# One folded projection for layer 1's first attention, and the 3x3 weights mixed on two engines

## The chip, the cores and the metric

The kernel runs on one core of one Trainium2 chip. The metric is the device time of that core in microseconds (us). The core has engines that run at once, each with its own queue of instructions that it works through in order: TensorE (PE, matrix products; its weight loads are listed apart as PEld), VectorE (DVE), ScalarE (ACT), GpSimd (POOL) and SyncE (SP, which here only starts transfers). GpSimd also starts transfers. Operands lie in SBUF, products land in PSUM.

## The reference

The input is x, (2, 256, 64, 64) in float32: two images ("batches") of 256 channels. Two layers each add something to x.

```python
x = x + layer0(gn(x))      # gn: group norm, 32 groups
x = x + layer1(gn(x))
```

Layer 0 is softmax attention with 8 heads over all 4096 positions. Layer 1, cut to what matters here:

```python
q = c1x1(x, conv1_w, conv1_b); k = c1x1(x, conv2_w, conv2_b); v = c1x1(x, conv3_w, conv3_b)
pos = tile(c1x1(loc, convp_w, convp_b))          # loc: column and row position, -1 to 1
fq = q * 64 ** -0.5 + pos
fk = k + pos
ctx = sa(blockify(fq), blockify(fk), blockify(v))     # 64 groups of 64 positions; the first attention
feats = bn_relu(c1x1(ctx, lr_W_w), ...)
qx, kx = two bn_relu(c1x1) each, of feats; vx = c1x1(feats, sr_fv_w)
out_att = bn_relu(c1x1(sa(qx, kx, vx), sr_W_w), ...)  # 64 groups again; the second attention
f_conv = mix of q, k, v by fc_w                       # 9 x 64 channels
out_conv = depthwise 3x3 of f_conv with dep_w
return rate1 * out_att + rate2 * out_conv
```

`sa` is softmax(q^T k * 256 ** -0.5) v. Within a group of 64 positions, a score is the product of one position's fq and another's fk. Adding to a position's scores a number that doesn't depend on the second position leaves its softmax unchanged. The mix by `fc_w` and the 3x3 behind it are linear in x, so both are one 3x3 over x whose weights follow from conv1_w, conv2_w, conv3_w, fc_w and dep_w.

## The kernel before, in words

Each batch is worked through in turn (the loop at L1245): the norm and projections of layer 0, the attention of layer 0 (`attention0`, over 1000 us of PE work a batch), then layer 1 in two parts. Channels lie on the 128 partitions in KC = 2 chunks; positions are cut into NT = 8 tiles of T = 512. Tile pools give out buffers: "w4" has 11 for working tiles, "wp" three for 256x256 matrices, PSUM eight banks in the first part of layer 1 and four in the second, beside four for the 3x3 (`pacc`).

**The first attention**, `layer1_first` (L1031). `to_groups` writes the normalised input into `xg`, ordered by group, so that `source(t)` gives tile t's 512 positions (8 groups) and all channels. `project` (L1064) multiplies it by w1 and by w2 (L1072) and adds bias and position by one more product of 16 rows, `st_posq` or `st_posk` with the tile's `loc` (L1076); for each of q and k and both 128-channel halves m that makes five products. ScalarE, and in batch 1 for k VectorE, copies q and k to SBUF. `group_attention` (L949) is a generator: scores `sp` (L977), each of 64x64, values `pvs` (L960), the softmax on VectorE with the exponential on ScalarE (L985 to L992); then, after the first `yield`, the transposes `at` (L997) and VectorE's copies `bd` (L1006); after the second, the context `pc` (L1015), which ScalarE turns into `feats` (L1026). `layer1_first` calls `project(t + 1, 0)` and `project(t + 1, 1)` at the two yields, so PE projects the next tile while VectorE works on this one's softmax. In float32 a product is two passes in the records.

**The 3x3's weights**, `conv_weights` (L760), run once, in batch 0. After some small preparation (L791 to L808), for both halves m of the output channels each of nine taps is a weighted sum of 12 rows of `wx` (128x256 each), a TENSOR_SCALAR (L818) and eleven SCALAR_TENSOR_TENSORs (L820), all on VectorE. Then come sums of taps for a transformed 3x3 with 16 weights in place of nine (L824 to L831), and a write to `wf_kept` in DRAM (L833). The two halves share `wx`, `taps` and `new_rows`, so the second loads its `wx` when the first is done with them.

**The second part**, `layer1_second` (L1146), works tile by tile: a q branch of two products (L1186, L1194), a k branch, the second attention, and in between steps of the 3x3, `conv()`: `conv_transform` on GpSimd (L884, L888) and `conv_step` on PE (L898) with its sums on VectorE (L904 to L925). In all there are 16 such steps. `fetch_conv_weights` (L845) loads `wf` and, in batch 0, turns its blocks with PE (L857). It is called at tile 0, and the steps go 3, 3, 2, 2, 2, 2, 2, 0 over the tiles. `results` holds each tile's output until the 3x3 has covered its rows.

**What sets the order.** In `with tc.manual_schedule(engines=...)` the named engines keep the order of the code; in the loop over tiles of the first attention, and in the second part, that is PE alone. The order of the other engines' queues is laid down before the run by a planner that takes an instruction when it expects it to be ready, earlier code first. So `conv_weights`, which comes after the attention in the code, fills VectorE's gaps between the softmax's instructions. `issue_after(done.ins)` (L1142) keeps it behind the last normalisation.

Of the kernel before, what the change touches and what calls it, by code (L numbers as in the profile page):

```python
# [17 lines left out]
P = 128  # L18
B, C, H, W = 2, 256, 64, 64
N = H * W  # L20
T = 512
# [19 lines left out]
def direct_layers(ctx: ExitStack, tc: tile.TileContext, a: dict, out: bass.AP, bad: bass.AP):  # L41
# [36 lines left out]

    ident = const.tile([P, P], F32, name="ident")
# [47 lines left out]
    def load_layer1():  # L127
# [5 lines left out]


        posk, posq = w4([4, C], "posk"), w4([4, C], "posq")
        nc.gpsimd.dma_start(out=posk, in_=a["posk"])
        nc.gpsimd.dma_start(out=posq, in_=a["posq"])
        rows = const.tile([4, 1], F32, name="pos_rows")
        nc.gpsimd.memset(rows, 8.0)
        nc.gpsimd.memset(rows[0:1, :], 1.0)  # L140
        nc.vector.tensor_scalar(posq, posq, rows, None, ALU.mult)
        def stack(name, rows):
            wts[name] = const.tile([16, C], F32R, name="st_" + name)
# [11 lines left out]
        later.append(lambda: (lambda: stack("posq", posq)))  # L155
        later.append(lambda: (lambda: stack("posk", posk)))
# [13 lines left out]
    kept_w = {name: dram.tile([P, KC, C], F32, name="kept_" + name) for name in ("w3", "fv")}  # L170
# [12 lines left out]
    def stack_positions(t):  # L183
# [14 lines left out]
        return halves_of  # L198

# [560 lines left out]
    def conv_weights():  # L760
# [49 lines left out]
        for m in range(2):  # L810
            for q in range(3):
                nc.gpsimd.dma_start(out=wx[:, 4 * q : 4 * q + 4, :], in_=a["wx"][q, m].rearrange("i p c -> p i c"))
            for tap in range(9):
                acc = taps[:, tap, :]
                for i in range(12):
                    src, s = wx[:, i, :], weff[:, m, i, tap : tap + 1]
                    if i == 0:
                        nc.vector.tensor_scalar(acc, src, s, None, ALU.mult)  # L818
                    else:
                        nc.vector.scalar_tensor_tensor(acc, src, s, acc, ALU.mult, ALU.add)  # L820
# [128 lines left out]
    def group_attention(nm, q, k, tokens, wv, out, busy=False, apart=False):  # L949
# [19 lines left out]
        if apart:  # L969
            values(0)  # L970

        sp = bank([P, 4, 64], f"sp_{nm}")
        for t in range(4):
            for c in range(KC):
                for par in range(2):
# [3 lines left out]
                        start=c == 0, stop=c == KC - 1,  # L979
                    )  # L980
        if not apart:
            values(0)
# [48 lines left out]
    def layer1_first(b, xts, put, check, st):  # L1031
# [19 lines left out]
        tiles, banks = {}, {}  # L1051
# [4 lines left out]
        def open_tile(t):  # L1056
            nt = f"lr_{b}_{t}"
            loc = w4([16, T], f"loc_{nt}", F32R)
            nc.sync.dma_start(
                out=loc.bitcast(F32), in_=loc_kept[:, :, :, t * T : (t + 1) * T].rearrange("l d r n -> (l d r) n")  # L1060
            )
            tiles[t] = loc, w4([P, KC, T], f"q_{nt}"), w4([P, KC, T], f"k_{nt}")

        def project(t, m, chunks):  # L1064

            loc, q, k = tiles[t]
            for nm, wt, pos, dst in (("q", "w1", "posq", q), ("k", "w2", "posk", k)):
                if chunks.start == 0:
                    banks[t, m, nm] = bank([P, T], f"p{nm}_lr_{b}_{t}_{m}")
                acc = banks[t, m, nm]  # L1070
                for c in range(chunks.start, chunks.stop):
                    nc.tensor.matmul(  # L1072
                        acc, wts[wt][:, c, m * P : (m + 1) * P], source(t)[:, c, :], start=c == 0, stop=False
                    )
                if chunks.stop == KC:
                    nc.tensor.matmul(acc, wts[pos][:, m * P : (m + 1) * P], loc, start=False, stop=True)  # L1076
                    if nm == "q":
                        nc.scalar.activation(dst[:, m, :], acc, AF.Copy, scale=0.125)
                    elif b == 0:
                        nc.scalar.copy(dst[:, m, :], acc)  # L1080
                    else:
                        nc.vector.tensor_copy(dst[:, m, :], acc)
# [5 lines left out]
        with tc.manual_schedule(engines={E.PE, E.Activation, E.DVE}):  # L1088
# [26 lines left out]
            open_tile(0)  # L1115
            for m in range(KC):
                project(0, m, slice(0, 1))
            for m in range(KC):
                project(0, m, slice(1, KC))
        with tc.manual_schedule(engines={E.PE}):  # L1120
            for t in range(NT):
# [5 lines left out]

                parts = group_attention(
# [697 lines left out]
```

## Time and profile before

Three runs took 3211.84 us (median; 3209.8 to 3215.32). The profile is of one further execution.

| | |
|---|---|
| profiled execution | 3213.2 us |
| its span, first to last instruction | 3211.4 us |
| mean granted clock of TensorE | 0.989 of full speed |
| PE busy | 3093.3 us, 96% |
| VectorE busy | 2487.2 us, 77% |
| ScalarE busy | 2316.5 us, 72% |
| GpSimd busy | 826.7 us, 26% |

Line numbers (L1072) are lines of the kernel before. In a timeline each row is a start in us, a length, the engine, the line, the operation, output<-inputs by the program's names, shape and count; in brackets stands the idle time ahead of it and what ended that. Several like instructions in a row are merged to one. A length can exceed the distance to the next start, since instructions overlap at their ends. A window's row gives the busy time of each engine in a stretch.

### The profile page before, as it was taken

To read this page: it belongs to the slowest core of one execution; us is meant where nothing else is said; L and a number is where in the kernel's file an instruction comes from. 1 tells how busy PE (TensorE), PEld (TensorE's weight loads), DVE (VectorE), ACT (ScalarE), POOL (GpSimd) and SP (SyncE) were. 2 spreads that over 40 slices of the span, in tenths; PEclk is the share of its full clock that TensorE was granted. 3 is DMA by queue.
4 is the path that set the end of the run, shared out by engine and by line. 5 is a ranking of instruction groups with operands and counts; after the bars stand their busy time and mean duration, and the time that the engine had idled before them with its cause. 6 is when DMAs were issued, how large, how long until landed. Compare 5 with 4: busy or idle time off the path is not lost. (4 is left out here: it accounts for less than half of the span.)

```text
span 3211.4 us, 62287 instructions
## 1 busy us (share of the span) xinstructions
PE 3093.3 (96%) x24889; PEld 1838.3 (57%) x24889; DVE 2487.2 (77%) x3223; ACT 2316.5 (72%) x2371; POOL 826.7 (26%) x918
## 2 busy tenths in 40 slices
PE   7899999999999989699998999999999999899998
PEld 4455555555555545466754555555555555456766
DVE  4599998999999988664445899889999999724543
ACT  2699999999999963422235999999999999724222
POOL 2122222222222210344200222222222222104530
PEclk9999999999999999899999999999999999999999
DMA  7968789689786741310049696897887966500000
GB/s 255 258 132 170 157 156 182 138 166 175 155 178 130 149 101 50 131 33 27 27 174 270 129 183 139 159 173 144 172 168 159 191 130 129 143 3 11 20 14 21
DMA packets 242957, 425.73 MB, mean 133 GB/s; under 512 B 99009, under 2 KB 110361, under 8 KB 240225
## 3 DMA queue, kind: packets, MB, share of 16 engines
q0 software_dynamic: 96176, 240.42, 39.0%
q1 hardware_dynamic: 146480, 181.25, 21.0%
q8 instruction: 197, 3.23, 0.4%
q14 instruction: 104, 0.84, 0.1%
HBM read 118.78 MB, written 67.86 MB: 58 GB/s over the span
## 5 line engine op out<-in xcount | busy, mean ns | idle before, releaser
L519 DVE TENSOR_TENSOR e<-e,es 128x1024 f32<-128x1024 f32 (+1 forms) x952 | 1035.9, 1142 | 96.9 <-ACT es L472 95.1
L482 PE MATMUL av<-es,v 128*32 128x256 f32 (+1 forms) x9644 | 747.6, 390 | 0.0
L519 DVE TENSOR_TENSOR e<-e,v 128x1024 f32<-128x1024 f32 (+1 forms) x640 | 675.9, 1108 | 54.4 <-ACT v L472 53.0
L472 ACT ACTIVATE es<-sa 128x1536 f32<-128x1536 f32 (+1 forms) x444 | 635.6, 1432 | 94.9 <-PE sa L466 54.2
L466 PE MATMUL sa<-q,k 128*128 128x512 f32 x1736 | 561.2, 430 | 13.0 <-issue 4.5
L482 PE MATMUL av<-v 128*32 128x256 f32 (+1 forms) x6228 | 506.9, 389 | 0.0
L482 PEld LDWEIGHTS av<-es,v 128*32 128x32 f32 x9644 | 316.5, 109 | 299.7 <-issue 161.3
L466 PEld LDWEIGHTS sa<-q,k 128*128 128x128 f32 x1736 | 280.0, 188 | 296.5 <-issue 142.4
L466 PE MATMUL sc<-q,k 128*128 128x512 f32 x1180 | 372.3, 397 | 10.1 <-ACT es L472 8.5
L466 PE MATMUL sb<-q,k 128*128 128x512 f32 x1180 | 371.1, 395 | 1.3 <-ACT es L472 1.3
L482 PEld LDWEIGHTS av<-v 128*32 128x32 f32 x6228 | 216.7, 109 | 179.3 <-issue 82.2
L472 ACT ACTIVATE es<-sc 128x1024 f32<-128x1024 f32 x296 | 306.9, 1037 | 7.8 <-DMA v<-es 7.8
L472 ACT ACTIVATE v<-sc 128x1024 f32<-128x1024 f32 x294 | 304.8, 1037 | 1.0 <-DMA acc<-v 1.0
L472 ACT ACTIVATE es<-sb 128x1024 f32<-128x1024 f32 x296 | 302.1, 1021 | 4.0 <-DMA acc<-es 3.9
L472 ACT ACTIVATE v<-sb 128x1024 f32<-128x1024 f32 x294 | 300.0, 1020 | 0.5 <-DMA acc<-v 0.5
L466 PEld LDWEIGHTS sc<-q,k 128*128 128x128 f32 x1180 | 210.3, 188 | 82.4 <-ACT es L472 21.0
L466 PEld LDWEIGHTS sb<-q,k 128*128 128x128 f32 x1180 | 221.0, 188 | 56.1 <-ACT es L472 3.5
L472 ACT ACTIVATE v<-sa 128x1536 f32<-128x1536 f32 (+1 forms) x146 | 209.2, 1433 | 35.0 <-PE sa L466 14.9
L898 PE MATMUL mm<-v,wf 128*128 128x256 f32 x1024 | 229.5, 382 | 3.7 <-DVE z L907 3.7
L529 POOL DMA_DIRECT2D es<-es x118 | 101.2, 858 | 484.8 <-ACT es L472 438.2
L888 POOL TENSOR_TENSOR v<-col 128x512 f32<-128x512 f32 x128 | 162.7, 1300 | 237.2 <-PE sp_sr L977 82.3
L898 PEld LDWEIGHTS mm<-v,wf 128*128 128x128 f32 x1024 | 194.4, 191 | 38.4 <-issue 7.7
(243 smaller groups left out, 3254.2 us busy)
## 6 DMA issues: line engine op xcount, KB each, us to landing
acc<-es POOLq DMA_DIRECT2D x130, 512.0 KB, 6.4
acc<-v POOLq DMA_DIRECT2D x84, 512.0 KB, 6.3
es<-es POOLq DMA_DIRECT2D x138, 256.0 KB, 4.3
v<-es POOLq DMA_DIRECT2D x134, 256.0 KB, 5.1
k<-wk_halves SPq DMA_DIRECT2D x64, 512.0 KB
q<-wq_halves SPq DMA_DIRECT2D x256, 128.0 KB
v<-v POOLq DMA_DIRECT2D x90, 256.0 KB, 5.0
es<-v POOLq DMA_DIRECT2D x86, 256.0 KB, 4.0
```

Source lines behind the costliest of these rows:

```text
L466: nc.tensor.matmul(sc[:, i, :], held["k", g // 2][:, j * P : (j + 1) * P], held["q", g, u // 2][:, u % 2, :], start=True, stop=True,)
L472: nc.scalar.activation(dst, sc[:, i : i + m, :], AF.Exp, scale=SC0)
L482: nc.tensor.matmul(dst[HD0 * u : HD0 * u + HD0, n], lhs, rhs(u)[:, n], start=start, stop=stop)
L519: nc.vector.tensor_add(dst[:, s, :], dst[:, s, :], src)
L529: nc.gpsimd.dma_start(out=dst, in_=src, accum_op=ALU.add)
L888: (nc.gpsimd.tensor_add if plus else nc.gpsimd.tensor_sub)(dst, rows(one), rows(two))
L898: nc.tensor.matmul(mm[:, m, r, :], wf[:, k, 4 * r + q, m * P : (m + 1) * P], v[r // 2][:, r % 2, k, :], start=k == 0, stop=k == KC - 1,)
```

## The change

**One projection.** In place of q and k there is y: the matrix g is formed once from w1 and w2, y = g applied to the input (plus position and bias rows), and the scores are products of y with the normalised input itself, `source(t)`. What the position adds on the keys' side needs two numbers a query, `ats`, which `at_grid` computes for four tiles at once, 32 columns each; `more` multiplies them by the group's positions (`grid`) onto the scores. Terms that are the same for all keys of a query are left out. `fold_scores` computes g at the start of batch 0 and keeps it in DRAM for batch 1. The plain w1 and w2 that it needs come row by row out of `wx`. Position loads go two tiles at a time.

**3x3 weights on two engines.** Taps 6, 7 and 8 are mixed on GpSimd, by a multiplication and an addition for each row; the other six stay on VectorE.

**A tile later.** In batch 0 `fetch_conv_weights` moves from tile 0 to tile 1, and the steps go 0, 3, 3, 3, 3, 2, 2, 0. Batch 1 keeps its steps.

```diff
     x_first = load_x(0)
+    by_out = {}
+    for name in ("w1", "w2"):
+        by_out[name] = wpool.tile([P, KC, C], F32, tag="wp", name=f"{name}_by_out")
+        for i in range(4):
+            for half in range(2):
+                r = 64 * (i % 2) + 32 * half
+                nc.sync.dma_start(
+                    out=by_out[name][r : r + 32, i // 2, :], in_=a["wx"][int(name == "w2"), half, i, 0:P:4, :]
+                )
+    place_rows = const.tile([4, C], F32, name="place_rows")
+    nc.sync.dma_start(out=place_rows, in_=a["posq"])
...
-        posk, posq = w4([4, C], "posk"), w4([4, C], "posq")
...
-        later.append(lambda: (lambda: stack("posq", posq)))
-        later.append(lambda: (lambda: stack("posk", posk)))
+        later.append(lambda: (lambda: stack("pos", wts["pos_rows"])))
...
+    def fold_scores():
+        wts["g"] = wpool.tile([P, KC, C], F32, tag="wp", name="wt_g_0")
...
+        for k in range(KC):
+            nc.tensor.transpose(pp[:, k, :], place_rows[:, k * P : (k + 1) * P], ident[0:4, 0:4])
+        nc.scalar.copy(place, pp)
+        pl = bank([4, C + 2], "pt_rows")
+        for dst, src in ((pl[:, 0:C], by_out["w2"]), (pl[:, C : C + 2], place[:, :, 1:3])):
+            for j in range(KC):
+                nc.tensor.matmul(dst, place[:, j, :], src[:, j, :], start=j == 0, stop=j == KC - 1)
+        nc.scalar.activation(rows[:, 0 : C + 2], pl, AF.Copy, scale=scale)
+        for k in range(KC):
+            pg = bank([P, C + 2], f"pt_g_{k}")
+            for dst, src in ((pg[:, 0:C], by_out["w2"]), (pg[:, C : C + 2], place[:, :, 1:3])):
+                for j in range(KC):
+                    nc.tensor.matmul(
+                        dst, by_out["w1"][:, j, k * P : (k + 1) * P], src[:, j, :], start=j == 0, stop=j == KC - 1
+                    )
+            nc.scalar.copy(wts["g"][:, k, :], pg[:, 0:C])
+            nc.scalar.copy(w_at[:, k, 0:2], pg[:, C : C + 2])
+        nc.sync.dma_start(out=kept_w["g"], in_=wts["g"])
...
-            for tap in range(9):
-                acc = taps[:, tap, :]
+            for tap in (6, 0, 1, 7, 2, 3, 8, 4, 5):
+                acc, term = taps[:, tap, :], new_rows[:, 0, :]
                 for i in range(12):
                     src, s = wx[:, i, :], weff[:, m, i, tap : tap + 1]
-                    if i == 0:
+                    if tap >= 6:
+                        nc.gpsimd.tensor_mul(acc if i == 0 else term, src, s.to_broadcast([P, C]))
+                        if i:
+                            nc.gpsimd.tensor_add(acc, acc, term)
+                    elif i == 0:
                         nc.vector.tensor_scalar(acc, src, s, None, ALU.mult)
                     else:
                         nc.vector.scalar_tensor_tensor(acc, src, s, acc, ALU.mult, ALU.add)
...
-        if apart:
+        first = apart or more and more[2]
+        if first:
             values(0)
...
-                        start=c == 0, stop=c == KC - 1,
+                        start=c == 0, stop=not more and c == KC - 1,
                     )
+            for par in range(2 if more else 0):
+                n0 = (4 * par + t) * 64
+                nc.tensor.matmul(
+                    sp[64 * par : 64 * par + 64, t, :], more[0][:, n0 : n0 + 64], more[1], start=False, stop=True
+                )
...
+            for c in range(chunks.start, chunks.stop):
+                nc.tensor.matmul(
+                    acc, wts["g"][:, c, m * P : (m + 1) * P], source(t)[:, c, :], start=c == 0, stop=False
+                )
+            if chunks.stop == KC:
+                nc.tensor.matmul(acc, wts["pos"][:, m * P : (m + 1) * P], loc_of(t), start=False, stop=True)
+                nc.scalar.activation(tiles[t][:, m, :], acc, AF.Copy, scale=0.125)
+        ats = cpool.tile([P, 2, T], F32, tag="col", name=f"at_{b}")
+        def at_grid(half):
+            pa = bank([P, T], f"pa_{b}_{half}")
+            for c in range(KC + 1):
+                for u in range(4):
+                    t, dst = 4 * half + u, pa[HD0 * u : HD0 * u + HD0, :]
+                    if c < KC:
+                        nc.tensor.matmul(dst, w_at[:, c, :], source(t)[:, c, :], start=c == 0, stop=False)
+                    else:
+                        nc.tensor.matmul(
+                            dst, wts["pos"][:, C : C + HD0].bitcast(F32), loc_of(t).bitcast(F32), start=False, stop=True
+                        )
+            nc.scalar.activation(ats[:, half, :], pa, AF.Copy, scale=0.125)
...
+            at_grid(0)
...
+                if t == 3:
+                    at_grid(1)
...
+        steps = (0, 3, 3, 3, 3, 2, 2, 0) if b == 0 else (3, 3, 2, 2, 2, 2, 2, 0)
...
-                if t == 0:
+                if t == steps.index(max(steps)):
                     wf = fetch_conv_weights(b)
-                if t + 1 < NT:
+                if steps[t] > 0:
                     conv()
...
-                if t + 1 < NT:
+                if steps[t] > 1:
                     conv()
...
-                if t < 2:
+                if steps[t] > 2:
                     conv()
...
+            if b == 0:
+                fold_scores()
...
-        load_set(b, ("w1", "w2", "w3"))
+        load_set(b, ("w3",) if b == 0 else ("g", "w3"))
```

## The prediction

> **What bounds the kernel now.** I read the page's first two parts, then the busy time of each stretch, then the timelines of TensorE, VectorE and GpSimd where the diff works. TensorE (PE) is busy 96% of the span. The stretches below are: up to batch 0's first attention of layer 1, that attention, the gap behind it, the rest of batch 0's layer 1, batch 1 up to its first attention, that attention, the end. Columns: window, length, then busy time (and instructions) of PE, PEld, DVE, ACT, POOL, the clock, DMA.
>
> ```profile
> 0.00:1180.10 1180.10, 1136.97 (x10444) 646.84 (x10444) 1019.27 (x1086) 1019.15 (x994) 307.15 (x395) 0.99 0.80 170
> 1180.10:1314.40 134.30, 130.63 (x688) 76.86 (x688) 121.71 (x342) 54.87 (x79) 3.04 (x9) 0.99 0.15 40
> 1314.40:1346.00 31.60, 7.40 (x17) 2.88 (x17) 16.96 (x12) 10.99 (x16) 25.53 (x16) 0.70 0.49 179
> ...
> 2788.00:2921.90 133.90, 130.47 (x688) 76.98 (x688) 42.53 (x91) 41.94 (x56) 0.79 (x6) 0.99 0.03 8
> ```
>
> Both first attentions are PE's: 134 us each, 130 busy. In batch 0 VectorE (DVE) is nearly as full, 121.7 of 134.3 us, as it also mixes the 3x3's weights; GpSimd (POOL) is empty. In the gap PE has 7.4 us of work in 31.6. PE's timeline for one tile of batch 0, then for the gap (start, length, what, idle before and its releaser):
>
> ```profile
> 1207.89 1.15 PE L977 MATMUL sp_lr<-k_lr,q_lr 128*64 128x64 f32 x32
> 1208.97 3.72 PE L960 MATMUL pvs_lr<-wt_w,xg 128*128 128x256 f32 x16
> 1212.53 1.88 PE L1072 MATMUL pq_lr<-xg,wt_w 128*128 128x512 f32 x4
> 1214.34 0.49 PE L1076 MATMUL pq_lr<-loc_lr,st_posq 16*128 16x512 f32 x1
> 1214.76 1.98 PE L1072 MATMUL pk_lr<-xg,wt_w 128*128 128x512 f32 x4
> 1216.67 0.49 PE L1076 MATMUL pk_lr<-loc_lr,st_posk 16*128 16x512 f32 x1
> 1217.10 0.44 PE L997 MATMUL at_lr<-ident,e_lr 128*128 128x128 f32 x2
> ...
> 1346.00 9.61 PE L857 MATMUL pw<-ident,wf 128*128 128x128 f32 x64 [23.79 <-DMA wf<-wf_kept]
> ```
>
> Tiles follow each other every 16.03 us (sp_lr at 1207.89 and 1223.92) with no idle. The second block's 23.79 us wait is for the finished 3x3 weights: their last sums, VectorE's L831, ended at 1331.36. Why they ended so late is the reading that decides my forecast. VectorE's last sums first alone (1251), then beside GpSimd's TENSOR_TENSORs, which are listed after them:
>
> ```profile
> 1251.86 1.09 DVE L831 TENSOR_TENSOR prep<-prep 128x256 f32<-128x256 f32 x3
> ...
> 1323.41 3.77 DVE L830 TENSOR_TENSOR prep<-prep 128x256 f32<-128x256 f32 x2
> 1327.10 4.26 DVE L831 TENSOR_TENSOR prep<-prep 128x256 f32<-128x256 f32 x3
> ...
> 1318.52 6.09 POOL L888 TENSOR_TENSOR v<-col 128x512 f32<-128x512 f32 x4
> 1326.97 5.50 POOL L888 TENSOR_TENSOR v<-col 128x512 f32<-128x512 f32 x4
> 1332.55 2.11 POOL L884 TENSOR_TENSOR col<-xp 128x1152 f32<-128x1152 f32 x1
> 1334.73 4.88 POOL L888 TENSOR_TENSOR v<-col 128x512 f32<-128x512 f32 x4
> ```
>
> Alone, three L831 take 1.09 us (0.36 each); beside L888 they take 1.42 each: every one waits for the GpSimd instruction in progress. GpSimd goes from 1.22 (4.88/4) to 1.38-1.52. They take turns, one for one: a turn costs GpSimd's instruction plus about 0.16 us.
>
> **What the Trainium skill says.** "SBUF — State Buffer", Who interferes with whom: a VectorE instruction with two SBUF inputs and a GpSimd instruction that reads SBUF exclude each other for a whole instruction. The trace agrees, as shown. "GPSIMD Engine Reference", 3.1 Elementwise: about 2.6 cycles an element for two inputs; at its 1.2 GHz an estimate of 0.55 us for 256 elements before dispatch. The trace has no such size. "TensorE: Matmul & The Clock Gate", Part 3: products on different 32-column strips run at once. The trace agrees: L482's rows products (128*32, 512 columns) come eight in 0.86 us (1156.73 to 1157.59), the time of one full product's two passes (4 in 1.81 at L1072).
>
> **The change part by part.** The sum is made against the profiled execution, 3213.2 us (span 3211.4 plus 1.8), which is 1.4 above the median of the runs.
>
> *One projection.* A tile's two blocks of q and k cost 2 x 4.57 us (1212.53 to 1217.10). One matrix instead of two takes half: -4.57 a tile, -36.6 a batch. Added: eight products of 32 rows to the scores, 16 passes where L977's 32 passes take 1.08, so 0.54; rows and strips change in between (bounds 0.5 to 1.4), I take 0.8, +6.4 a batch. The at_grid products: two halves of 12, four side by side, 6 x 0.43 = 2.6, with two changes of shape 2.9, +5.8 a batch. Net -24.4 a batch where PE stays the bound: a period of about 12.2. Copies, four a tile, become two on an engine busy 40%: nothing. The position loads become four instead of eight; SP has little to do there: nothing.
>
> Does the softmax still fit? Between sp and at stay 3.56 + 2.28 = 5.84 us. In batch 1, where VectorE is free, the chain L985 to L992 takes 2.45 (2881.20 to 2883.65); from at to pc the uncovered last tile took 1.81 (2916.69 to 2918.50), the cover becomes 0.27 + 2.28 = 2.55. So batch 1 gives its 24.4.
>
> *3x3 weights on two engines.* VectorE keeps 132 of 198 SCALAR_TENSOR_TENSORs (two SBUF inputs; 0.48 long, 0.395 from start to start, 12 of them from 1218.46 to 1223.22) and 12 of 18 TENSOR_SCALARs (0.27). GpSimd gets 3 taps x 23 x 2 halves = 138 instructions of 128x256. Their length: at least half of L888's 1.22, 0.61; on the line through 1.22 (512) and 2.11 (1152) 0.87; each waits for the one before, up to 0.1 more. I take 0.82, range 0.61 to 0.97. A turn is then 0.98, and VectorE gets one per turn: per half 66 x 0.98 + 6 x 0.27 + some 2 us of softmax outside turns in each of three tiles = 72 us, where nine taps alone took about 56 (1190.5 to 1246, softmax included).
>
> VectorE's queue is in order, and its order is drawn up before the run, as if nothing collided: with tiles every 12.2 us some 21 mixing instructions stand between two softmaxes (33 did in 16.03). At 0.98 these are 21 us, plus 3.7 of softmax: 24-25 us a tile. PE then waits for e and bd, which it hardly did. So batch 0 loses its -24.4 and more: three tiles in the first half's 72 us, to 1262. Then the last sums (7 us) and the reload of wx for the second half; before, 14.8 us from 1245.6 to 1260.4, and now softmaxes of PE's late tiles stand between: 28, to 1290. Second half 72, to 1362; last sums 7 alone or 17 beside GpSimd (before: 17), say 10; write, issue and load as before, 14.6 (1331.4 to 1346.0): wf at about 1387.
>
> *Used a tile later.* What PE reaches in the meantime: the first attention ends between 1340 and 1374 (1312 before), feats 2.2, tile 0 without 3x3 work about 24 (the last tile of batch 1, also without: 3180.1 to 3203.2), the q branch of tile 1 7: 1373 to 1407. The 3x3 starts at the later of both, about 1397. Before, PE stood at 1346.0 with 21 us more to do: tile 0's k branch and attention without 3x3, 13.9 (of 1362.35 to 1383.36), and tile 1's q branch, 7. Equal point 1367: **+30 us** in batch 0, all included. If nothing collided, these two edits would save the 23.79 us wait; that is where the gain goes. Batch 1's steps are as before.
>
> *The rest.* Folding the weights at the start: six 256-column products and small ones, some 3-5 us of PE, partly in its idle first 21 us; SP issues 17 small loads behind x, but no longer w1 and w2: +3 (0 to 8). Two more results of tiles 0 to 2 hold w4 buffers until tile 2 is done, so GpSimd's transforms start later: +3 (0 to 6). The posq/posk work was hidden under layer 0: nothing.
>
> Sum: -24.4 + 30 + 3 + 3 = +12: 3225 for the profiled execution, 3224 for a median.
>
> **Rivals.** *No collision that matters* (ends on the other side): if the turns cost VectorE nothing, both first attentions give 24.4; GpSimd's halves end at 1247 and 1318, wf at 1342 against the equal point 1367: -25. Total -25 - 24 + 6, 3170. For it: L820 itself never ran beside GpSimd. Against: L830, L831 and L919 did, and doubled or worse. It turns at a GpSimd instruction near 0.6: turns of 0.77, batch 0 about +12, total within 0.2%. *GpSimd at 0.97 and the second half queued late*: turns of 1.13, 11 us more a half and a stall chain of 20: 3260. *Batch 1's softmax is late too* (bd misses its cover by 2 us in 8 tiles): +16, 3240; the 0.7 us of slack speaks against.
>
> **How the numbers follow.** Forecast (collision, batch 0 pays more than batch 1 gains) and its two worse rivals 0.58; balance within 0.2%, about what a measurement of this kernel can tell from no change, 0.14; little collision 0.28. So faster 0.28, same 0.14, slower 0.58. Slower cases run to 3265; to leave out no more than 2 in 10 the low end reaches into the rival, 3172. The forecast's own range is 3210 to 3262.
>
> **What would show it.** Right: in batch 0's first attention VectorE's L820 near 1.0 us instead of 0.48, PE waiting for DVE e_lr and bd_lr, tiles of 20 us or more while GpSimd mixes, but 12.2 in batch 1; wf later than 1370. Wrong: L820 still at 0.48 beside GpSimd, GpSimd's instructions under 0.6, or PE's start of the 3x3 blocks before 1350.

## The result

The changed kernel takes 3198.77 us (median of four runs, 3195.62 to 3200.03); the kernel before, run beside it, 3210.82. The ratio is 0.9958, with a 95% interval of 0.9941 to 0.9976: faster by 0.42%. The forecast was slower, 3224. The profiled execution took 3200.0 us, its span 3198.2.

The profile after, in five stretches: up to batch 0's first attention, that attention, then up to the first 3x3 block, the rest of batch 0's layer 1 with batch 1 up to its first attention, that attention. (Line numbers from here on are of the changed kernel: mixing on VectorE is L868 and L870, on GpSimd L864 and L866; the sums L874 to L881; scores L1029, their additions from the grid L1035; `pw` L907.)

```profile
0.00:1184.35 1184.35, 1140.07 (x10470) 650.38 (x10471) 1017.40 (x1084) 1021.41 (x1000) 307.39 (x400) 0.99 0.76 170
1184.35:1345.06 160.71, 130.63 (x785) 84.37 (x785) 148.26 (x291) 47.09 (x66) 103.48 (x147) 0.84 0.14 41
1345.06:1379.03 33.97, 31.11 (x115) 17.01 (x116) 2.71 (x7) 18.81 (x27) 16.25 (x11) 0.90 0.31 124
1379.03:2794.33 1415.30, 1385.30 (x11660) 826.63 (x11658) 1151.87 (x1368) 1089.53 (x1088) 384.44 (x417) 0.99 0.65 147
2794.33:2908.97 114.64, 111.79 (x784) 72.32 (x785) 32.00 (x75) 43.12 (x58) 0.78 (x6) 0.98 0.03 7
```

Batch 1's attention fell from 133.9 to 114.6 us, with PE busy throughout. Batch 0's, the same products, grew from 134.3 to 160.7: there the lack is VectorE (busy for 148.3 us, in which its instructions' waits for GpSimd count as busy). The stretch behind it is as long as the old gap, but PE is busy in 31.1 of 34.0 us instead of 7.4 of 31.6: it now holds tile 0's k branch and attention and tile 1's q branch. From stretch to stretch the ends shift like this:

| stretch | before, us | after, us | difference |
|---|---|---|---|
| start to the first product of batch 0's attention | 1180.1 | 1184.4 | +4.2 |
| from there to batch 1's norm for layer 0 | 455.3 | 461.0 | +5.7 |
| from there to the first product of batch 1's attention | 1152.6 | 1149.0 | -3.6 |
| batch 1's first attention | 133.9 | 114.6 | -19.3 |
| to the end | 289.5 | 289.2 | -0.2 |

Together -13.2, the difference of the spans. PE in batch 0's attention, the rows ahead of which it waited:

```profile
1209.71 0.66 PE L1055 MATMUL at_lr<-ident,e_lr 128*128 128x128 f32 x2 [6.99 <-DVE e_lr L1050]
1226.69 0.66 PE L1055 MATMUL at_lr<-ident,e_lr 128*128 128x128 f32 x2 [2.60 <-DVE e_lr L1050]
...
1288.46 3.75 PE L1073 MATMUL pc_lr<-bd,vs_lr 128*128 128x128 f32 x16 [3.08 <-DVE bd L1064]
1308.48 2.02 PE L1073 MATMUL pc_lr<-bd,vs_lr 128*128 128x128 f32 x16 [1.27 <-DVE bd L1064]
...
1379.03 1.15 PE L907 MATMUL pw<-ident,wf 128*128 128x128 f32 x9
```

PE waits for softmax (`e_lr`) and copies (`bd`), as forecast, and not at all for `wf` in the last row: the weights were there first. A wait can cost more than its own length: the sixteen products of L1073 take 3.75 us after one and 2.02 after another. The granted clock of these stretches tells them apart: 0.52 from 1288.46 to 1302.10, 0.96 from 1302.40 to 1323.70, 1.00 from 1262 to 1282, where PE hardly waits. "TensorE: Matmul & The Clock Gate", section "HAM oscillation — how this bites in real kernels", has the rule that gaps in the array's work of over some 3.4 us bring its clock down; the windows agree in kind (clock 0.84, 130.6 us for 785 products, against 0.98 and 111.8 us for the same products in batch 1). The wait ahead of the 3.75 was only 3.08 us.

VectorE and GpSimd in the middle of the first half of the mixing:

```profile
1234.38 6.64 DVE L870 SCALAR_TENSOR_TENSOR prep<-prep 128x256 f32<-128x256 f32 x8
1240.94 0.70 DVE L868 TENSOR_SCALAR prep<-prep 128x256 f32<-128x256 f32 x1
...
1235.08 0.79 POOL L866 TENSOR_TENSOR prep<-prep 128x256 f32<-128x256 f32 x1
1235.95 0.67 POOL L864 TENSOR_TENSOR prep<-prep 128x256 f32<-128x256 f32 x1
1236.70 0.80 POOL L866 TENSOR_TENSOR prep<-prep 128x256 f32<-128x256 f32 x1
```

Eight VectorE instructions take 6.56 us from start to start, 0.82 each, where twelve took 4.76 (0.395 each) before. GpSimd's go at the same pace: a pair in 1.62 us (1235.08 to 1236.70). They take turns one for one; a turn, from one start of VectorE's to the next, is 0.81 us. How much of it GpSimd loses these rows don't show: in this trace each of its mixing instructions runs beside VectorE's, and its recorded length can hold a wait (e12 has some that run alone).

In the same 61 us of the first half's mixing (61.32, from 1195.23 to 1256.55; 60.61 in e1 below) VectorE goes through 72 mixing instructions and three softmaxes here, through 108 and five without GpSimd. A third of the mixing is taken off it, and the half gets no shorter.

### The profile page after: what moved, and what is told of

It is laid out like the page before. It is cut to its first block, busy times and chain, and to the rows that moved or that the text cites. A ratio compares the mean times of both kernels' runs of the same rounds, so it can differ in the third digit from the quotient of the medians.

```text
span 3198.2 us, 62765 instructions
## 1 busy us (share of the span) xinstructions
PE 3077.4 (96%) x25107; PEld 1844.3 (58%) x25107; DVE 2492.2 (78%) x3133; ACT 2311.5 (72%) x2365; POOL 927.3 (29%) x1061
## 5 line engine op out<-in xcount | busy, mean ns | idle before, releaser
L938 POOL TENSOR_TENSOR v<-col 128x512 f32<-128x512 f32 x128 | 162.1, 1293 | 217.3 <-PE sp_sr L1029 49.5
```

The lines of the kernel that those rows point to most:

```text
L938: (nc.gpsimd.tensor_add if plus else nc.gpsimd.tensor_sub)(dst, rows(one), rows(two))
```

## The experiments

"Layer 1 of batch 0" runs from the first product of its attention to batch 1's norm, so it takes in all that happens in front of the 3x3. Ratios are to the kernel before, with 95% intervals; stretches are from one profiled execution each.

| run | what is different | median us | ratio | first attention, batch 0 / 1 | layer 1 of batch 0 |
|---|---|---|---|---|---|
| before | | 3210.8 | 1 | 134.3 / 133.9 | 455.3 |
| after | | 3198.8 | 0.9958 [0.9941, 0.9976] | 160.7 / 114.6 | 461.0 |
| e1 | after, nine taps on VectorE | 3180.5 | 0.9906 [0.9891, 0.9921] | 116.3 / 114.3 | 439.1 |
| e2 | after, weights used at tile 0 | 3198.3 | 0.9966 [0.9952, 0.9979] | 157.7 / 114.3 | 457.9 |
| e3 | one projection alone (e1 and e2) | 3205.3 | 0.9981 [0.9974, 0.9987] | 116.6 / 113.9 | 464.5 |
| e4 | after, fold moved | 3188.2 | 0.9927 [0.9914, 0.9941] | 157.6 / 114.7 | 456.0 |
| e5 | two engines alone | 3233.3 | 1.0077 [1.0063, 1.0090] | 180.3 / 135.2 | 473.0 |
| e6 | a tile later alone | 3191.3 | 0.9943 [0.9929, 0.9957] | 134.8 / 135.2 | 434.2 |
| e7 | after, one tap on GpSimd | 3191.4 | 0.9939 [0.9925, 0.9952] | 134.7 / 114.8 | 448.8 |
| e8 | e1, transforms held (one sum) | 3185.0 | 0.9926 [0.9913, 0.9940] | 115.2 / 114.8 | 436.9 |
| e9 | after, scores in alternating order | 3199.9 | 0.9957 [0.9943, 0.9971] | 159.0 / 111.3 | 458.2 |
| e10 | e1, e4 and e9 | 3164.9 | 0.9843 [0.9830, 0.9857] | 111.8 / 111.0 | 436.7 |
| e11 | e10, transforms held (four sums) | 3158.7 | 0.9831 [0.9818, 0.9844] | 114.4 / 110.2 | 425.6 |
| e12 | after, GpSimd's instructions halved | 3218.3 | 1.0021 [1.0014, 1.0028] | 174.0 / 114.2 | 470.8 |

**The theory** that the prediction leaves: while GpSimd mixes, the turns cost batch 0's VectorE more than the offload saves it. **The rival**: the split is what pays, and the sign of the forecast was wrong because of that.

**e1, nine taps on VectorE.**

```diff
-                    if tap >= 6:
+                    if tap >= 9:
```

> The changed kernel with all nine taps of the 3x3's weights on VectorE. Theory A (the turns between VectorE and GpSimd are what stretches batch 0's first attention to 160.7 us): VectorE's mixing goes back to 0.395 us an instruction, the first attention of batch 0 falls to 115-118 us and ends near 1300, the weights are done near 1350 and TensorE waits for them at most some 10-30 us in front of the 3x3; about 3170 us, 29 under the changed kernel. Rival B (the split relieves VectorE, which could not mix nine taps in a shorter attention): the attention stays above 130 us or the weights come after 1375, and the time is 3199 or more.

The split costs: without it the time is 3180.5 us, 18 less, with intervals that don't overlap (the profiled execution, 3173.6, lies 7 under its own median). VectorE runs at its own pace again:

```profile
1230.64 4.84 DVE L870 SCALAR_TENSOR_TENSOR prep<-prep 128x256 f32<-128x256 f32 x12
```

The window of this attention:

```profile
1183.03:1299.28 116.25, 112.09 (x785) 72.47 (x785) 102.19 (x293) 46.91 (x65) 3.05 (x9) 0.97 0.14 40
```

PE's waits in front of the 3x3:

```profile
1339.33 0.69 PE L1055 MATMUL at_sr<-ident,e_sr 128*128 128x128 f32 x2 [22.61 <-DVE e_sr L1050]
...
1354.78 7.21 PE L907 MATMUL pw<-ident,wf 128*128 128x128 f32 x64 [2.42 <-DMA wf<-wf_kept]
```

With nine taps VectorE is busy for 102.2 us of 116.3, with six for 148.3 of 160.7. But PE now waits 22.61 us in tile 0, for a softmax that stands in VectorE's queue behind the last sums. And those collide anew, with GpSimd's transforms for the 3x3 (L938), which start earlier as the attention ends earlier. VectorE, and below it GpSimd at the same time:

```profile
1318.39 1.47 DVE L870 SCALAR_TENSOR_TENSOR prep<-prep 128x256 f32<-128x256 f32 x1
1319.79 1.47 DVE L880 TENSOR_TENSOR prep<-prep 128x256 f32<-128x256 f32 x1
1321.18 1.47 DVE L870 SCALAR_TENSOR_TENSOR prep<-prep 128x256 f32<-128x256 f32 x1
...
1316.88 5.49 POOL L938 TENSOR_TENSOR v<-col 128x512 f32<-128x512 f32 x4
```

Turns of 1.39 us, with a GpSimd instruction of 1.37. That these keep e1 above the expected 3170 is tried in e8 and e11. But two such streams don't always take turns. The transform ahead of these, and VectorE's mixing in the middle of it:

```profile
1300.66 16.14 POOL L934 TENSOR_TENSOR col<-xp 128x1152 f32<-128x1152 f32 x1 [6.06 <-ACT xp L1235]
...
1304.87 6.41 DVE L870 SCALAR_TENSOR_TENSOR prep<-prep 128x256 f32<-128x256 f32 x16
```

Its like takes 2.1 us in e11 (L936). Here it stood while VectorE's mixing went by at its own 0.395 us an instruction, and ran only after the sum (L874) that VectorE began at 1313.85; the turns begin there. What decides which of the two happens, no run separates.

**e2, weights used at tile 0.**

```diff
-        steps = (0, 3, 3, 3, 3, 2, 2, 0) if b == 0 else (3, 3, 2, 2, 2, 2, 2, 0)
+        steps = (3, 3, 2, 2, 2, 2, 2, 0)
```

> The changed kernel with the 3x3's weights fetched and used at tile 0 again in batch 0. Theory A (the weights are the bound only by a few us, since the stretched attention ends at 1345 anyway): TensorE meets the 3x3 at about 1355 and waits 5-20 us for the weights, whose last part is written near 1345 and lands near 1360; no 3x3-free tile 0 has to be bridged later, so the time is 3199 to 3206. Rival B (using them a tile later carries the gain): 20 us or more worse, above 3215.

3198.3 us: with the split in, using the weights a tile later is worth nothing that this shows. PE started `pw` at 1356.31, after a wait of 5.78 us for `wf`. So the weights were ready near 1356 with the split.

**e3, one projection alone** (both edits above).

> The changed kernel with nine taps on VectorE and the weights used at tile 0: the one projection and the folded weights alone. Theory A: the first attention of batch 0 lasts 115-118 us, but the weights are done near 1350 as in the kernel before, TensorE waits some 42 us for them, and batch 0 gains nothing; batch 1 gains 19 us as in the changed kernel; about 3196 (3190 to 3202). Rival B: the one projection also gains in batch 0, about 3175.

3205.3: a gain of 6 us where some 15 were expected, and batch 0 does worse than before (464.5 us against 455.3). Batch 1 gained its 20. In batch 0 the shorter attention leads PE to the 3x3 sooner and to a longer wait:

```profile
1360.68 9.04 PE L907 MATMUL pw<-ident,wf 128*128 128x128 f32 x64 [52.48 <-DMA wf<-wf_kept]
```

The weights also came 15 us later than in the kernel before (1346.0). The first half of the mixing, with five softmaxes in it instead of four, ended at 1255.26 instead of 1245.54; in the second half the transforms met VectorE's last mixing instructions, as in e1, so that it took 69.1 us instead of 53.8, and the sums behind it, which met them before, gave a part of that back. Between e3 and e1, where only the step at which the weights are used differs, 25 us lie: with a short attention, "a tile later" pays. Between e3 and e2, where only the split differs, the split gains 7 us (the two intervals just overlap). If PE waits at the 3x3 anyway, a slower attention costs little. And as the transforms wait for ScalarE's `xp`, which comes with the end of the attention, they start at 1344.07 in e2, behind the last sums, and at 1301.82 in e3, ahead of them.

**e4, the fold behind the first projection.**

```diff
-            if b == 0:
-                fold_scores()
             mean, rstd = group_stats(xts, f"l0_{b}")
...
             held = project0(b, xn, w0)
+            if b == 0:
+                fold_scores()
```

> The changed kernel with the folding of the weights moved from ahead of the first group norm to behind the first projection in batch 0. Theory A (the fold stands in TensorE's queue ahead of the norm's product and holds back the first projection by 8 us): the first product of the projection starts at 22-25 us instead of 29.6, and the time is 4 to 8 us less, 3191 to 3195. Rival B (the eight us are the loads', or are made up later by a wait that is there anyway): within 2 us of 3199.

3188.2, 10.6 less than the changed kernel. PE at the start of the changed kernel:

```profile
20.62 0.34 PE L227 MATMUL pt_place<-ident,place_rows 4*128 4x4 f32 x2 [20.62 <-DMA place_rows<-in_posq_dram]
...
26.61 0.36 PE L333 MATMUL pm_l<-mv_l,group 128*128 128x2 f32 x2
...
29.63 16.72 PE L418 MATMUL p_wk<-xn,wqk 128*128 128x512 f32 x32 [1.44 <-DVE xn L368]
```

And in e4:

```profile
16.26 0.58 PE L333 MATMUL pm_l<-mv_l,group 128*128 128x2 f32 x2 [16.26 <-DVE mv_l L330]
...
21.92 15.42 PE L418 MATMUL p_wk<-xn,wqk 128*128 128x512 f32 x32 [3.65 <-DVE xn L368]
```

The fold itself is 6 us of PE. But it stands in PE's queue ahead of the norm's product, which was ready by 16, and it waits until 20.62 for the last of its loads. Of the 8 us at the first projection 4.2 are left at the first attention in the changed kernel. The rest comes back in layer 0's attention (up to the first product of layer 1's), 1066.2 us in the changed kernel and 1071.0 before; over all profiled kernels with the one projection it took 1064.8 to 1070.2, in the three without it 1070.0 to 1071.0. PE's waits for ScalarE's `es` there fell from 6.45 to 4.67 us, but came to 7.34 in e8; whether the change does any of that stays open.

**e5, two engines alone**, on the kernel before: the diff's hunk in `conv_weights` and nothing else.

> The kernel before with three of the nine taps mixed by GpSimd, and nothing else. Theory A (each GpSimd instruction holds VectorE up for about 0.4 us, and two of them replace one VectorE instruction of 0.4 us): VectorE's stream is as long as in the changed kernel, the first attention of batch 0 goes from 134 to 150-160 us though its tiles are TensorE's 16 us each, TensorE meets the 3x3 near 1360 instead of 1346, batch 1 is as before; 3220 to 3228. Rival B (a third less work for VectorE brings the weights earlier): the weights land before 1340, 3205 or less.

3233.3, slower by 0.77%, more than expected. The attention takes 180 us. VectorE's planned order holds more mixing instructions between two softmaxes here (30 to 33 where the changed kernel has 22 to 24), as the tiles were planned longer. PE's waits, at the places where they were largest:

```profile
1298.04 0.69 PE L1001 MATMUL at_lr<-ident,e_lr 128*128 128x128 f32 x2 [5.56 <-DVE e_lr L996]
...
1322.09 0.79 PE L1080 MATMUL pq_lr<-loc_lr,st_posq 16*128 16x512 f32 x1 [5.82 <-DMA loc_lr<-loc_kept]
```

The second is a load of positions that stands in SP's queue behind the writes of the sums, which wait for VectorE.

**e6, a tile later alone**, on the kernel before: the steps and the fetch of the diff.

> The kernel before with the 3x3's weights fetched and used a tile later in batch 0, and nothing else. Theory A (this alone fills the wait of 23.8 us in front of the 3x3 with tile 0's attention): TensorE comes to the 3x3 near 1350 having done 21 us more work than before; 3190 to 3195. Rival B (tile 0's softmax stands in VectorE's queue behind the last sums, so that the wait comes back in front of that): a wait for VectorE of 10 us or more in tile 0 and 3200 or more.

3191.3, as expected by theory A. That is 7 us less than with the whole change by the medians and 5 by the ratios, whose intervals overlap. PE's wait for the softmax in tile 0 is 2.79 us and there is none for `wf`. Theory A doesn't name all of the cause: VectorE's last sums (L831) ended at 1318.86 instead of 1331.36, as they kept GpSimd's first transform out (recorded with 6.27 us from 1314.58) and stayed at some 0.34 us each. How much of the 18 us is due to that, no run separates. PE's rows:

```profile
1333.43 0.69 PE L997 MATMUL at_sr<-ident,e_sr 128*128 128x128 f32 x2 [2.79 <-DVE e_sr L992]
...
1346.06 7.15 PE L857 MATMUL pw<-ident,wf 128*128 128x128 f32 x64
```

**e7, one tap on GpSimd** (`if tap >= 8`).

> The changed kernel with one tap on GpSimd instead of three (23 GpSimd instructions a half instead of 69). Theory A (every GpSimd instruction costs VectorE about 0.41 us, and every pair of them saves it 0.395): VectorE's stream in the first attention is 5 us a half longer than with none and 10 us a half shorter than with three; the attention lasts 116 to 130 us, the time lies between that of no tap (3180) and three (3199), about 3184. Rival B (the offload helps as long as GpSimd isn't the later of the two): less than 3178.

3191.4, between none (3180.5) and three (3198.8), and more than expected. Batch 0's attention takes 134.7 us, 18.4 more than with no tap; three taps add 44.5. With 46 GpSimd instructions a tap that is 0.40 and 0.32 us for each, near what a turn adds to a VectorE instruction (0.81 less 0.395, 0.415). The expectation had set the VectorE instructions saved against that. But the growth holds PE's slower products too (busy for 121.0 us against 112.1 in e1), so it is no clean measure of a turn. A part comes back behind the attention, where PE's wait in tile 0 is 14.98 us instead of e1's 22.61. Neither one tap nor three pays here.

**e8, the transforms held back.** A GpSimd copy that reads a last sum of the weights stands ahead of the first transform. In e8, on e1, it reads a sum of the fourth row; in e11, on e10, of all four rows. The diff is e11's.

```diff
+        last = const.tile([P, 4, 1], F32, name="last_sum")
+        kept["last"] = nc.gpsimd.tensor_copy(last, new_cols[:, :, 1, 0:1])
         edges = const.tile([P, 2, 5], F32, name="edges")
...
-        ahead = {0: conv_transform(b, xp, *turns[0])}
+        if b == 0:
+            with tc.issue_after(kept["last"].ins):
+                ahead = {0: conv_transform(b, xp, *turns[0])}
+        else:
+            ahead = {0: conv_transform(b, xp, *turns[0])}
```

> The changed kernel with all nine taps on VectorE, as in the first experiment, and in addition GpSimd's first transforms of the 3x3's input held back until VectorE's last sum of the weights (a GpSimd copy of one column that reads that sum stands ahead of them). Theory A (the turns with the transforms stretch VectorE's last 20 mixing and sum instructions from 0.4 to 1.4 us, and tile 0's softmax is queued behind them): TensorE's wait of 22.6 us for that softmax falls to below 8, the 3x3 starts near 1342 instead of 1354.8, and the time is 8 to 13 us less than in the first experiment, about 3169. Rival B (the transforms, held back by some 10 us, come late for the 3x3 or for its next step): TensorE waits for the transforms and the time is 3178 or more.

A miss, by its design: the fourth row's sums came early in VectorE's planned order, so the copy ran at 1324.46, and VectorE's remaining sums until 1342 met the transforms as before; PE's wait for the softmax was 17.15 us. 3185.0 against e1's 3180.5 says nothing against the theory nor for it: layer 1 of batch 0 took 436.9 us against 439.1, and it began 7 us later.

**e9, scores in alternating order.** In every second quarter the products of 32 rows (the grid's) come ahead of those of 128 rows.

```diff
-            for c in range(KC):
-                for par in range(2):
+            ahead = t % 2 == 1
+            for early in ((True, False) if more else (False,)):
+                for par in range(2 if more and early == ahead else 0):
...
+                        start=ahead, stop=not ahead,
...
+                for c in range(KC if not more or early != ahead else 0):
+                    for par in range(2):
```

> The changed kernel with the score products in alternating order: in every second quarter of a tile the products of 32 rows come ahead of those of 128 rows, so that four changes of shape a tile take the place of seven. Theory A (a change of shape costs TensorE 0.12 us each way, which makes 0.9 us of the 1.49 that the scores grew by): scores 2.57 us to about 2.15, tiles of batch 1 12.85 to about 12.45, 3 to 4 us less in batch 1, nothing in batch 0, where VectorE sets the pace; 3195. Rival B (the products of 32 rows are slow by themselves): scores at 2.5 us or more, time within 1.5 us of the changed kernel's 3199.

The scores behave as theory A says, the time is inconclusive. PE in a tile's scores in the changed kernel, which go on like this until 2833.04:

```profile
2830.47 0.45 PE L1029 MATMUL sp_lr<-xg,y 128*64 128x64 f32 x8
2830.85 0.33 PE L1035 MATMUL sp_lr<-grid,at 32*64 32x64 f32 x4
2831.11 0.45 PE L1029 MATMUL sp_lr<-xg,y 128*64 128x64 f32 x8
```

In e9, until 2834.40:

```profile
2832.27 0.45 PE L1037 MATMUL sp_lr<-xg,y 128*64 128x64 f32 x8
2832.65 0.45 PE L1030 MATMUL sp_lr<-grid,at 32*64 32x64 f32 x8
2833.03 0.69 PE L1037 MATMUL sp_lr<-xg,y 128*64 128x64 f32 x16
```

Scores fell from 2.57 to 2.13 us and batch 1's attention by 3.3. Eight passes of 128 rows take 0.38 us from start to start, sixteen take 0.62, so eight more are 0.24 and the 0.14 left over is put down to the change of shape; grid passes, four in 0.26 and eight in 0.38, give 0.14 too. The median is 3199.9 all the same: batch 1's attention began 2.5 us later than in the changed kernel, as much as one run differs from another.

**e10, e1 with e4 and e9**, and **e11**, the same with the hold on all four sums.

> Three edits of the experiments together on the changed kernel: nine taps on VectorE, the fold of the weights behind the first projection, the score products in alternating order. Theory A (they act in different places, so the gains add: 18 and 11 us measured, 3 to 7 us expected of the third in both batches): 3162 to 3169. Rival B (the gain of the alternating order or of the fold is given back in front of the 3x3 of batch 0, where the weights are the bound): above 3170.

> The same three edits, and GpSimd's first transforms of the 3x3's input held back until all four of VectorE's last sums of the weights are done (the hold of the experiment before read only one of the four, and that one came early). Theory A (without the transforms beside them VectorE's last instructions take 0.4 us instead of 1.4, so tile 0's softmax behind them comes up to 20 us earlier): TensorE's wait for that softmax falls below 10 us and the time is 8 to 15 us less than with the three edits alone. Rival B (the transforms come late instead): TensorE waits for them in front of the first product of the 3x3 and the time is the same within 3 us.

e10 gave 3164.9, the gains added. e11 gave 3158.7, 1.7% under the kernel before. That is 6 us less than e10, short of the 8 to 15 expected (the intervals of the two overlap; layer 1 of batch 0 fell from 436.7 to 425.6 us). PE's wait for tile 0's softmax in e10:

```profile
1328.94 0.69 PE L1058 MATMUL at_sr<-ident,e_sr 128*128 128x128 f32 x2 [21.40 <-DVE e_sr L1053]
```

In e11:

```profile
1327.33 0.69 PE L1060 MATMUL at_sr<-ident,e_sr 128*128 128x128 f32 x2 [7.20 <-DVE e_sr L1055]
```

VectorE's mixing and sums in e11, where e1's took turns of 1.39 us:

```profile
1312.63 0.47 DVE L870 SCALAR_TENSOR_TENSOR prep<-prep 128x256 f32<-128x256 f32 x1
1313.03 0.41 DVE L879 TENSOR_TENSOR prep<-prep 128x256 f32<-128x256 f32 x1
```

The wait fell from 21.40 to 7.20 us, and a mixing instruction takes 0.40 us again. Some 6.5 us go back at another place, a wait of 3.60 us for ScalarE's `hq_sr` and slower products behind it; and `pw` starts without a wait for `wf`. This is the fastest kernel of the study.

**e12, GpSimd's instructions halved.** Each instruction of 256 columns becomes two of 128; the work is the same.

```diff
-                        nc.gpsimd.tensor_mul(acc if i == 0 else term, src, s.to_broadcast([P, C]))
-                        if i:
-                            nc.gpsimd.tensor_add(acc, acc, term)
+                        for h in (slice(0, C // 2), slice(C // 2, C)):
+                            dst = acc if i == 0 else term
+                            nc.gpsimd.tensor_mul(dst[:, h], src[:, h], s.to_broadcast([P, C // 2]))
+                            if i:
+                                nc.gpsimd.tensor_add(acc[:, h], acc[:, h], term[:, h])
```

> The changed kernel with every mixing instruction of GpSimd cut into two of 128 columns (276 instead of 138 in the attention of batch 0, the same work on VectorE). Theory A (VectorE waits for the GpSimd instruction in progress, so a turn is that instruction's length and about 0.14 us): an instruction of 128 columns takes about 0.35-0.45 and a turn 0.5-0.6 us instead of 0.81; VectorE's mixing beside GpSimd goes at that pace, the attention lasts 130-145 us instead of 160.7, though GpSimd's half takes longer, 69 x 2 x 0.55 = 76 us instead of 55; 3185 to 3200. Rival B (a turn has a fixed price, whatever the instruction's length): VectorE stays at 0.8 us beside GpSimd for twice as many turns, GpSimd's half takes 110 us, and the time is above 3225.

On the turn the theory held, on the time it didn't. VectorE's mixing, and its wait for GpSimd in the second half:

```profile
1198.44 4.09 DVE L872 SCALAR_TENSOR_TENSOR prep<-prep 128x256 f32<-128x256 f32 x7
...
1346.10 0.96 DVE L876 TENSOR_TENSOR prep<-prep 128x768 f32<-128x768 f32 x1 [19.97 <-POOL prep L868]
```

PE's wait for VectorE behind it:

```profile
1354.36 0.69 PE L1057 MATMUL at_lr<-ident,e_lr 128*128 128x128 f32 x2 [20.97 <-DVE e_lr L1052]
```

GpSimd beside that mixing, then while VectorE stands still (up to 1219.19):

```profile
1200.47 1.24 POOL L868 TENSOR_TENSOR prep<-prep 128x128 f32<-128x128 f32 x2
1201.67 1.12 POOL L866 TENSOR_TENSOR prep<-prep 128x128 f32<-128x128 f32 x2
1202.74 1.05 POOL L868 TENSOR_TENSOR prep<-prep 128x128 f32<-128x128 f32 x2
...
1217.48 0.86 POOL L868 TENSOR_TENSOR prep<-prep 128x128 f32<-128x128 f32 x2
1218.30 0.75 POOL L866 TENSOR_TENSOR prep<-prep 128x128 f32<-128x128 f32 x2
1219.02 0.87 POOL L868 TENSOR_TENSOR prep<-prep 128x128 f32<-128x128 f32 x2
```

Seven VectorE instructions in 4.01 us, a turn of 0.57 instead of 0.81: its length follows GpSimd's instruction. GpSimd pays as well. Beside VectorE four of its instructions take 2.27 us from start to start, 0.57 each, alone 1.54, 0.385 each; the recorded lengths, 0.39 (multiplication) and 0.45 us (addition) alone, grow by the wait. But GpSimd's half takes 65 us instead of 55, VectorE is through with its own taps sooner, and stops at a sum that needs GpSimd's; the softmaxes queued behind that sum stop too. So the attention takes 174.0 us. In the first half a 16.61 us wait for a position load behind SP's writes comes on top. With the weights used a tile later the split loses either way: by turns, or by a queue that stands for the other engine.

## Why the prediction was wrong

**The step that failed** is "3x3 weights on two engines", in its sizes, and through it "used a tile later": +30 us for batch 0 was +5.7. The mechanism was as forecast (turns one for one, PE waiting for `e_lr` and `bd`). Two terms were too large, and a third followed from them:

- A turn was taken at 0.98 us, from a GpSimd instruction of 0.82 and 0.16 for the rest. It measured 0.81. GpSimd's instructions are recorded with 0.675 us (multiplication) and 0.789 (addition), waits included; with e12's loss of 0.57 - 0.385 = 0.185 a turn one alone would be some 0.62 us, an estimate, at the low end of the range of 0.61 to 0.97. VectorE's mixing of a half took 61 us instead of 72 (1195.23 to 1256.55, the first sums in between), GpSimd's 55.
- From the first half's end to the second's start was put at 28 us and took 15.5 (1256.55 to 1272.00). That is the reload of `wx` as before (14.9, 1245.54 to 1260.43); the softmaxes that were to stand in between didn't hold it up. So the second half began at 1272 instead of 1290 and ended at 1334 instead of 1362.
- The last sums took 9 us against 10, and `wf` was ready near 1356 (e2; in the changed kernel the last sum ended at 1342.39 and the load was issued at 1345.56), not at 1387. PE, with the attention ended at 1345.06 (forecast 1340 to 1374), came to the 3x3 at 1379.03 without a wait; the forecast of 1397 had two parts, and only PE's own was real.

The prediction's rival without collision named the point at which it turns: turns of 0.77 us, batch 0 at +12, no change in total. Measured were 0.81 and, with the start, +9.9; the total came out 13 lower. The rival's own cause was wrong: the collisions are there, and without the split (e1) the time is 18 us lower again. That the sign came out as this rival's owes nothing to its reason.

**One projection**: forecast -24.4, measured -19.3 in batch 1. The period was 12.85 us (`py` at 2865.16, 2878.01, 2890.86) instead of 12.2. The extra of the scores was 1.49 a tile (2.57 against 1.08), not 0.8, just outside the bounds of 0.5 to 1.4: the seven changes of shape cost about 0.14 us each (e9). That is 8 x 0.69 = 5.5 us, all of the 5.1 missing. `at_grid` took 2.85 us against 2.9. That the softmax still fits held: PE waits for it in batch 1 only in the last tile (1.42 us). "TensorE: Matmul & The Clock Gate", Part 3, on strips that run at once, gave the passes rightly; the price of a change of shape had to be measured.

**Batch 0's tiles** came every 20 us or so (`sp_lr` at 1196.01, 1215.67, 1235.2), not 24 to 25. With 0.81 in place of 0.98 the prediction's own sum, 21 turns and 3.7 us of softmax, gives 20.7. What the forecast hadn't: behind some of the waits the products are slower, at a lower granted clock. PE's 785 products took 130.6 us there (clock 0.84) and 112.1 in e1 (0.97). How much of that 18.5 us lies beside VectorE's work, no run separates.

**The rest**: the start was +8.0 at the first projection and +4.2 at the first attention, against +3; the wait for loads was seen, the place in PE's queue ahead of the norm was not. Layer 0 of batch 1 gave 3.6 us that nothing in the prediction stands for (over all profiles that stretch took 1146.1 to 1153.6 us). No sign of the +3 for w4 buffers was found.

**The total**: from the forecast's +12 to -13, the 25 us are -24.3 of batch 0, +5.1 of batch 1, +1.2 of the start, -3.6 of batch 1's layer 0, -3 of the buffers. Of the signs named, "tiles of 20 us or more", "PE waiting for e_lr and bd_lr" and "12.2 in batch 1" came nearly so, "L820 near 1.0 us" was 0.82, and "wf later than 1370" failed, the one that the sign hung on.

**What pays in the change** is thus not what one would read from its sum: the later use of the weights alone gives 0.57%, the one projection alone 0.19%, both together (e1) 0.94%, and the split takes 0.52% of that back. With the weights used at tile 0 the split gives 0.15% instead (e3 to e2).

## What to carry to other kernels

Before moving instructions from VectorE to GpSimd, count turns, not work: where the two engines take turns, each GpSimd instruction costs VectorE the turn less its own instruction, here 0.81 less 0.395 us, and two of them replaced one of 0.395. Shortening a stretch moves what comes next forward, into whatever runs there: here transforms into the last sums, until they were held back (e11). And a preparation put ahead in an in-order queue costs its loads' delay on top of its own length (here from 16.3 to 20.6 us, and 6 us).

## What the runs showed of the hardware

- "SBUF — State Buffer", Who interferes with whom, has the two engines exclude each other. The runs add who pays: beside each other they alternate one for one, and both pay. VectorE's instruction goes from 0.395 to 0.81 us; GpSimd's, at 128 columns, from 0.385 to 0.57 (e12). At 128 columns of GpSimd's the turn is 0.57, at 256 it is 0.81, at 512 it is 1.39. They don't always alternate: in e1 a stream of VectorE's mixing, at 0.395 us each, kept a GpSimd instruction out for some 13 us (1300.66 to 1313.85).
- VectorE's TENSOR_SCALAR, with one tensor and one scalar a partition, also took turns (L868): 0.35 us long alone, 0.70 to 0.82 beside GpSimd. The softmax's reductions and the subtraction from PSUM stayed at 0.41 to 0.43.
- Beside VectorE's mixing a GpSimd multiplication of 128x256 takes 0.675 us and an addition 0.789 (means of the changed kernel). Of 128x128 they take 0.39 and 0.45 alone, and a turn of 0.57 in place of 0.81: halving the columns saves less than a third of the turn.
- Changing between products of 128 and of 32 rows costs TensorE about 0.14 us each time, an estimate from the passes in e9.
